# Transformer block, MLP stage: row moves on the sync queue in written order, later stores, and first inner sums made one stage earlier

## The chip, the cores and the metric

The kernel runs on one core of one Trainium2 chip. A core has TensorE (PE in the profile; its weight loads are PEld), VectorE (DVE), ScalarE (ACT), GpSimd (POOL) and SyncE (SP), and 16 DMA engines that they share. Each engine runs its own list of instructions in order and waits on semaphores for the others. DMAs are started by an instruction of SP, POOL or ACT; those of SP go into one hardware queue (q1 in the profile), those of POOL into a software queue (q0). The metric is the device time in microseconds of one execution; three runs of the kernel before gave 3164.5 to 3169.8 us, median 3166.41 us.

## The reference, cut to what matters

```python
mod = silu(c) @ w_ada + b_ada                         # six vectors of 576 per batch
x   = x + g_msa * (attention(ln(x) * (1 + sc_msa) + sh_msa) @ w_proj + b_proj)
xn2 = ln(x) * (1 + sc_mlp) + sh_mlp                   # x: 2 x 2048 rows of 576, float32
h   = gelu(xn2 @ w1 + b1)                             # w1: 576 x 2304
out = x + g_mlp * (h @ w2 + b2)                       # w2: 2304 x 576
```

Everything is float32. The change lies in the last three lines, the MLP; what is ahead of it (norms, attention with 16 heads of 36, projection) is the same in both kernels.

## The kernel before, in words

**First MLP half (`xn2`, `h`).** The 4096 rows are cut into 8 blocks `n` of 512 rows (`NB`), the 2304 hidden features into 2 times 9 chunks `f` of 128 (`HF` = 9). A job is one pair (n, f): it makes the chunk `f` of both feature halves for 512 rows, by Strassen's scheme in Winograd's form: seven products instead of eight for a 2 by 2 blocked product. There are 72 jobs, run two to a turn of the loop. Of a job, `whole_part` and `last_part` are TensorE's part (L1982, L1996); seven sums go to one PSUM side of three banks (`m0` or `m1`, jobs alternate) and a bank `one` that both sides share. `gelu_stored` (L2004 to L2026) then works on one of three SBUF tiles `cs0` to `cs2`, number job mod 3: ScalarE copies product 1 out of PSUM (L2008), VectorE adds up the rest (L2009 to L2016), ScalarE applies GELU to two halves (L2020), GpSimd makes the four sums of the hidden block that the second half needs (L2022 to L2025), and SP stores all seven 128x256 pieces, 896 KB, to `operands[n]` in DRAM (L2026). So PSUM of job j is wanted again by job j+2, and `cs` of job j by the ScalarE copy of job j+3.

**Rows for the next block.** While block m is worked on, the four 128-row tiles of block m+1 are made ready, by `ahead(job)`: *load* the rows from DRAM (L1026), *turn* them (layer norm by statistics on VectorE, a square root on ScalarE with its table load (L281), a scaling and a 32x32 transpose on VectorE (L1042), then four DMAs that write the squares to DRAM (L1047)), *read* the turned rows back (L1055, L1057: one DMA of 256 KB, two of 32 KB), and *modulate* them on ScalarE (L1064, L393, L394; six instructions). For tile i of block m+1 these stand at job 9m+2i plus an offset: load -5, turn -2, read 0, modulate 1. All its DMAs are GpSimd's. At a block's end `token_sums` (L1952 to L1955) makes the block's sums on VectorE.

**Weights for the second half.** `weights_made` cuts w2 into seven combinations with VectorE and keeps them in DRAM (`w_kept`): two of its 63 steps follow each two jobs. Each of four rounds of 13 steps has one step of four loads, one of three and one of four stores of 504 KB (L2073), all on SP, and eight of VectorE sums; a last, shorter round and the loading of the products 1, 2 and 6 into `w_first` follow.

**Second MLP half (`out`).** 56 products (n, m): for each block the seven outer Strassen products, each of which is again done by seven inner ones (`multiplied`, L2201 and L2210). The operand of a product, 1152 KB, is loaded from `operands` into one of three places in turn (L2125); its four inner sums (`sums_made`, L2183 to L2186) are made one product ahead, by GpSimd for even products and VectorE for odd ones. `combined_blocks`, `finished` and the branches between them add results up on VectorE and send four quadrants per block to `out` (L2247, on GpSimd).

**What sets the order.** Inside this part TensorE and VectorE follow the order of the code. The order on ScalarE, GpSimd and SP is chosen by the framework's scheduler, which places an instruction by what it estimates. Tiles are reused by address: `hs`, the pool of the second half, lies where the row blocks, the last rows of w1 and the `cs` tiles of the first half were, and a first write there waits for the last use.

## Time and profile before

The profiled execution took 3162.72 us, of which the span from its first to its last instruction is 3160.9 us. The table is of that execution. A job's or product's time is TensorE's, from its first matmul to that of the next.

| what | from | us |
|---|---|---|
| first MLP half, 72 jobs | 2122.86 to 2701.64 | 578.78 |
| a job when nothing is waited for (2666.64 to 2673.64) | | 7.00 |
| waits of TensorE in the first half, sum | | 51.7 |
| product 0 of the second half | 2701.64 to 2721.04 | 19.40 |
| a product when nothing is waited for (2721.04 to 2728.88) | | 7.84 |
| from the last matmul's end to the end of the span | 3152.41 to 3160.90 | 8.49 |

How to read the rows that follow: a row of the timeline has start and duration in us, engine, line, operation, written tile <- read tiles, the count of merged instructions (the duration then spans them all), and in brackets how long the engine had been idle and who released it. A row of a table by stage has the busy time of each engine, the granted TensorE clock as a share of the full one, the share of time in which the DMA engines were busy, and GB/s.

### The profile page before, as it was taken

The page shows a single profiled execution, that of the slowest core. Times are in us where ns is not written, and L with a number is a line of the kernel's source. Part 1 is how long each engine was busy: PE and PEld are TensorE (multiplying, and loading weights), DVE is VectorE, ACT ScalarE, POOL GpSimd, SP SyncE. Part 2 cuts the span into 40 slices and gives each one's busy share as a digit, 9 for nine tenths or more (in the row PEclk, how much of TensorE's full clock was granted, in tenths as well). Part 3 has the DMA queues.
Part 4 walks back from the last instruction along what each step waited for, and adds up shares of the span by engine and source line. Part 5 has one row for each costly group of instructions (what it writes and reads, how often), then busy time and mean ns, then how long its engine had stood idle before and what let it go on. Part 6 is the DMA issues. An engine that isn't in the chain of part 4 may idle for free.

```text
span 3160.9 us, 51170 instructions
## 1 busy us (share of the span) xinstructions
PE 3075.0 (97%) x19079; PEld 1917.0 (61%) x19079; DVE 1677.7 (53%) x2521; ACT 1493.4 (47%) x2909; POOL 1081.0 (34%) x1407
## 2 busy tenths in 40 slices
PE   8999999999999999999999999999888999899998
PEld 6883333333334788433333333378777878899998
DVE  6773444444444566434444434365555654576766
ACT  2336666766666033566666666614444543000000
POOL 4550100123321454100001111026666664555554
PEclk9999999999999999999999999999999999999999
DMA  5873332233342744311122222166776678765554
GB/s 151 189 139 88 100 88 57 74 94 91 95 112 55 230 89 81 79 45 44 46 55 80 80 65 74 33 201 175 216 225 186 184 223 286 278 201 191 202 188 144
DMA packets 368585, 413.53 MB, mean 131 GB/s; under 512 B 169288, under 2 KB 297864, under 8 KB 360200
## 3 DMA queue, kind: packets, MB, share of 16 engines
q1 hardware_dynamic: 311776, 286.35, 30.6%
q0 software_dynamic: 47120, 118.51, 14.2%
q10 hardware_dynamic: 9432, 5.31, 0.7%
q8 instruction: 153, 2.51, 0.3%
q14 instruction: 104, 0.85, 0.1%
HBM read 244.81 MB, written 154.75 MB: 126 GB/s over the span
## 4 chain that ended last, share of the span: by engine, by line
PE 81%; DMA 6%; POOL 4%; issue 3%; DVE 3%; ACT 3%; SPq 0%; POOLq 0%; DVEq 0%; ACTq 0%
PE b L1549 29%; PE b L1536 20%; PE b L2201 12%; PE s L1143 6%; PE s L1229 5%; PE m L1982 3%; DMA xnt<-turned 2%; PE s L411 2%; PE b L2210 2%; DMA parts<-turned 1%; DMA turned<-squares 1%; PE s L1145 1%; ACT cs L2020 1%; PE s L1235 1%; POOL cs L2023 1%
## 5 line engine op out<-in xcount | busy, mean ns | idle before, releaser
L1540 ACT ACTIVATE pt<-b 128x512 f32<-128x512 f32 x2048 | 1057.3, 610 | 482.1 <-PE b L1549 267.6
L1549 PE MATMUL b<-pt,vt 128*64 128x512 f32 x4096 | 935.0, 598 | 1.8 <-ACT pt L1540 1.8
L1549 PEld LDWEIGHTS b<-pt,vt 128*64 128x64 f32 x4096 | 271.8, 136 | 583.9 <-issue 437.7
L1536 PE MATMUL b<-qm,km 32*128 32x512 f32 x4096 | 563.8, 613 | 0.0
L1601 DVE TENSOR_TENSOR ot<-b,ot 128x512 f32<-128x512 f32 x192 | 132.8, 691 | 586.7 <-PE b L1549 586.7
L1536 PE MATMUL b<-qe,ke 16*128 16x512 f32 x2048 | 420.1, 791 | 0.0
L1536 PEld LDWEIGHTS b<-qm,km 32*128 32x128 f32 x4096 | 190.6, 184 | 271.2 <-ACT pt L1540 211.3
L1982 PE MATMUL m<-xnt,wb 128*128 128x256 f32 x864 | 217.0, 388 | 22.1 <-DVE cs L2016 21.2
L1143 PE MATMUL s<-wq,xnt 128*128 128x288 f32 x864 | 226.7, 406 | 2.0 <-ACT xnt L400 2.0
L1568 DVE RECIPROCAL den<-den 128x512 f32<-128x512 f32 x64 | 213.5, 3336 | 10.4 <-DMA den<-den_dram 10.4
L2218 ACT COPY one<-b 128x144 f32<-128x144 f32 x56 | 15.6, 278 | 425.1 <-PE b L2201 409.9
L1064 ACT ACTIVATE xnt<-xnt,mod 128x128 f32<-128x128 f32 x244 | 101.0, 482 | 238.2 <-DMA xnt<-turned 146.0
L1982 PE MATMUL m<-s,wb 128*128 128x256 f32 x864 | 210.9, 380 | 0.0
L1982 PEld LDWEIGHTS m<-xnt,wb 128*128 128x128 f32 x864 | 161.7, 194 | 47.3 <-DVE cs L2016 26.1
L1599 DVE COPY ot<-b 128x512 f32<-128x512 f32 x64 | 44.3, 692 | 273.5 <-PE b L1549 273.5
L1143 PEld LDWEIGHTS s<-wq,xnt 128*128 128x128 f32 x864 | 158.0, 190 | 37.5 <-ACT xnt L400 2.7
L1982 PEld LDWEIGHTS m<-s,wb 128*128 128x128 f32 x864 | 165.0, 191 | 22.7
L1536 PEld LDWEIGHTS b<-qe,ke 16*128 16x128 f32 x2048 | 106.7, 184 | 114.0 <-issue 113.3
L1658 POOL DMA_DIRECT2D spare<-in_x_dram x32 | 17.7, 554 | 442.7 <-DVE met L796 442.7
L2020 ACT ACTIVATE cs<-cs,b_sb 128x512 f32<-128x512 f32 x144 | 99.4, 719 | 106.0 <-DVE cs L2015 105.7
L2009 DVE TENSOR_TENSOR cs<-m,cs 128x512 f32<-128x512 f32 x72 | 49.2, 683 | 185.9 <-ACT cs L2008 145.7
L817 POOL DMA_DIRECT2D km<-qk x56 | 28.1, 502 | 322.8 <-PE b L1536 321.3
(305 smaller groups left out, 4672.0 us busy)
## 6 DMA issues: line engine op xcount, KB each, us to landing
operands<-cs SPq DMA_DIRECT2D x72, 896.0 KB
operand<-operands SPq DMA_DIRECT2D x37, 1152.0 KB
wb<-operands SPq DMA_DIRECT2D x19, 1152.0 KB
spare<-in_x_dram POOLq DMA_DIRECT2D x64, 288.0 KB, 3.1
x_dram<-spare POOLq DMA_DIRECT2D x64, 288.0 KB, 2.5
qm<-qk SPq DMA_DIRECT2D x256, 64.0 KB
den<-den_dram SPq DMA_DIRECT2D x128, 128.0 KB
w_kept<-w_first SPq DMA_DIRECT2D x31, 504.0 KB
```

Of the source, the lines that this page charges most:

```text
L411: nc.tensor.matmul(outs[a], stationary(k, a), moving(k, a), start=(first and k == 0), stop=(not first and k == FULL - 1),)
L1064: nc.scalar.activation(part, part, AF.Identity, **affine(which, k, b))
L1143: nc.tensor.matmul(out_a, full[:, k, :], wq[:, k, f], start=k == 0, stop=False)
L1229: nc.tensor.matmul(out[m], x_[:, k, :], w_(k), start=k == 0, stop=k == 1 and m == 6)
L1536: nc.tensor.matmul(ps, k[r, keys], q[r, :], start=first, stop=not first)
L1540: nc.scalar.activation(pt[:, h, :], banks[2 * c + h], AF.Exp, scale=SCALE)
L1549: nc.tensor.matmul(acc[64 * h : 64 * h + 64, :], vt[:, v0 : v0 + 64], pt[:, h, :], start=pt is pts[0][0], stop=pt is pts[-1][0],)
L1568: nc.vector.reciprocal(den, den)
L1601: nc.vector.tensor_tensor(ot, acc, ot, ALU.add)
L1982: nc.tensor.matmul(out_m[m], wb[:, f, slot[m], k, :], moving[m](k), start=k == 0 and m in (1, 2, 5, 6), stop=k == 1 and m == 1,)
L2020: nc.scalar.activation(part, part, AF.Gelu, bias=b1_sb[:, g : g + 1])
L2201: nc.tensor.matmul(out_m[m], stationary[m][:, c, :], w[:, FULL * (m - 1) + c, :], start=a == 0 and c == 0, stop=ends and c == FULL - 1 and ...
```

## The change

Six things are altered, all in the MLP.

1. Load, turn and read of the rows ahead go through SP instead of GpSimd, and modulate stands one job later (offset 2).
2. `gelu_stored` is split: `hidden_made` computes, and `hidden_stored`, which stores job j, is written two jobs later, behind the row moves of that place.
3. The loop of the first half is put under a manual schedule for SP, GpSimd and ScalarE: they follow the written order. SP also does in the second half.
4. The first three inner sums of product 0 are made by GpSimd in the first half, at job 36, in a tile of their own (`first_sums`); the fourth comes at the start of the second half, on VectorE.
5. The operand of product 1 is loaded in the first half, at job 64, to the front of the used-up weights `wb`; the weights of products 5 and 7 follow it there two jobs later than before (jobs 66 and 68), those of product 4 come behind product 1 of the second half, those of product 3 behind product 2.
6. The very last product has its own end, `last_finished`: its inner products 4 and 3 get a PSUM bank each, everything that doesn't need them is added first, and the two halves of the result leave separately through SP.

```diff
@@ rows ahead
-            for what, todo in at(turn=-2, read=0, modulate=1, load=-5):
+            for what, todo in at(turn=-2, read=0, modulate=2, load=-5):
-                    rows_ahead[todo] = mlp_loaded(*todo, nc.gpsimd)
+                    rows_ahead[todo] = mlp_loaded(*todo, nc.sync)
-                    rows_ahead[todo] = tile_turned(rows_ahead[todo], nc.gpsimd)
+                    rows_ahead[todo] = tile_turned(rows_ahead[todo], nc.sync)
-                    turned_loaded(block, cols, rows_ahead.pop(todo), nc.gpsimd)
+                    turned_loaded(block, cols, rows_ahead.pop(todo), nc.sync)
@@ stores
-            nc.sync.dma_start(out=operands[n][:, :, f, :].rearrange("i p c -> p i c"), in_=cs)
+        def hidden_stored(job):
+            if job >= 0:
+                n, f = divmod(job, HF)
+                nc.sync.dma_start(out=operands[n][:, :, f, :].rearrange("i p c -> p i c"), in_=css[job % 3])
@@ the loop (new text)
+        with tc.manual_schedule(
+            engines={mybir.EngineType.SP, mybir.EngineType.Pool, mybir.EngineType.Activation}
+        ):
+            for job in range(0, NB * HF, 2):
+                (n0, f0), (n1, f1) = divmod(job, HF), divmod(job + 1, HF)
+                ahead(job)
+                hidden_stored(job - 2)
+                whole_part(n0, f0, 0)
+                if f1 == 0:
+                    token_sums(n1)
+                last_part(n0, f0, 0)
+                ahead(job + 1)
+                hidden_stored(job - 1)
+                hidden_made(n0, f0, 0)
+                whole_part(n1, f1, 1)
+                last_part(n1, f1, 1)
+                if f1 == HF - 1 and n1 + 1 < NB:
+                    token_sums(n1 + 1)
+                hidden_made(n1, f1, 1)
+                for _ in range(2):
+                    if job >= 2 and making_weights:
+                        making_weights.pop(0)()
+                if job == 2 * HF:
+                    operand_loaded(0)
+                if job == 4 * HF:
+                    sums_made(0, slice(0, 3))
+                at_job = job + 1 - (NB - 1) * HF
+                if at_job == 2:
+                    operand_loaded(1)
+                for i, m in enumerate((5, 7)):
+                    if at_job == (4, 6)[i]:
+                        weights_loaded(m, weight_spots[m])
+        for job in (NB * HF - 2, NB * HF - 1):
+            hidden_stored(job)
@@ start of the second half
-        for i in (1, 2):
-            operand_loaded(i)
-        w_last = hs.tile([P, WSIZE], F32, name="w_last")
-        weights_loaded(3, w_last)
+        operand.append(hs.tile([P, HF, PAIR], F32, name="operand2"))
+        operand_loaded(2)
+        weight_spots[3] = hs.tile([P, WSIZE], F32, name="w_last")
+        sums[0].append(hs.tile([P, FULL, P], F32, name="fourth"))
+        sums_made(0, slice(3, 4))
@@ loop of the second half
+            quadrant = {2: (0, 0), 7: (1, 1), 4: (1, 0), 3: (0, 1)}.get(m)
+            xr = residual_rows(n, *quadrant, gate_bias) if quadrant else None
+            out_m, outs = multiplied(i)
+            operand_loaded(i + 3)
+            if i in (1, 2):
+                weights_loaded((4, 3)[i - 1], weight_spots[(4, 3)[i - 1]])
+            if i + 1 == len(products):
+                last_finished(z12, out_m, outs, n, *quadrant, xr, gate)
+                break
@@ end of the last product
+            tt(z, z, r, ALU.add)
+            tt(z, z, part, ALU.mult)
+            tt(z, z, xr, ALU.add)
+            for i, m, cols, op in ((1, 4, slice(0, QUARTER), ALU.subtract), (0, 3, slice(QUARTER, HALF), ALU.add)):
+                tt(r[:, i, cols], out_m[m], part[:, i, cols], ALU.mult)
+                tt(z[:, i, cols], z[:, i, cols], r[:, i, cols], op)
+                nc.sync.dma_start(out=rows_of(n, t, a, out)[:, i], in_=z[:, i])
```

What the built programs have at three places follows; tiles keep their numbers.

SP around job 18, block 2 (L2026 stores hidden blocks before, L2031 in the change). Before, SP carries stores and weights alone:

```order
L2026 DMA operands1_17603<-cs2_17979 128x7x256
L2026 DMA operands1_17603<-cs0_17977 128x7x256
L2026 DMA operands1_17603<-cs1_17978 128x7x256
L2026 DMA operands1_17603<-cs2_17979 128x7x256
L2026 DMA operands2_17604<-cs0_17977 128x7x256
```

In the change, the same stretch, from the read of one tile (`turned42`) at job 18 on:

```order
L1055 DMA xnt1_17620<-turned42_18768 128x4x128
L1057 DMA parts1_17621<-turned42_18768 64x128 x2
L1047 DMA turned43_18869<-squares_18867 32x18x32 x4
L2031 DMA operands1_17603<-cs1_17979 128x7x256
L1026 DMA xt1_17971<-x1_dram_190 128x576
L2031 DMA operands1_17603<-cs2_17980 128x7x256
L2152 DMA operand0_17965<-operands0_17602 128x2304
L1055 DMA xnt1_17620<-turned43_18869 128x4x128
L1057 DMA parts1_17621<-turned43_18869 64x128 x2
L1047 DMA turned44_18968<-squares_18966 32x18x32 x4
L2031 DMA operands2_17604<-cs0_17978 128x7x256
```

The store of job 16 (`cs1`) now stands behind the four writes of a turn; that of job 17 (`cs2`) has only a load ahead of it. In blocks of even number a turn stands in the first half of a loop turn, ahead of both stores; in blocks of odd number it stands between the two.

ScalarE early in block 0 (jobs 4 and 5, `cs1` and `cs2`). Before:

```order
L281 ACT_TABLE_LOAD
L281 ACTIVATE std_18189<-mv_18187,eps6_65 128x1
L1064 ACTIVATE xnt1_17620<-xnt1_17620,mod_91 128x128 x4
L393 ACTIVATE parts1_17621<-parts1_17621,mod_91 128x128
L394 ACTIVATE tail1_17622<-parts1_17621,mod_91 128x128
L2008 COPY cs1_17978<-one_17985 128x256
L2020 ACT_TABLE_LOAD
```

In the change:

```order
L1064 ACTIVATE xnt1_17620<-xnt1_17620,mod_91 128x128 x4
L393 ACTIVATE parts1_17621<-parts1_17621,mod_91 128x128
L394 ACTIVATE tail1_17622<-parts1_17621,mod_91 128x128
L281 ACT_TABLE_LOAD
L281 ACTIVATE std_18190<-mv_18188,eps6_65 128x1
L2009 COPY cs1_17979<-one_17986 128x256
L2021 ACT_TABLE_LOAD
```

Before, the tile that is modulated here was read back by a DMA of the preceding job; in the change its read belongs to job 2, two jobs earlier, and the modulation stands ahead of the root of the next turn.

GpSimd at the handover to the second half (operand0 is product 0's operand, operand2 product 2's; `cs2` holds job 71). Before:

```order
L2025 TENSOR_TENSOR cs2_17979<-cs2_17979 128x256
L2183 TENSOR_TENSOR sums_21336<-operand0_17965 128x512
L2185 TENSOR_TENSOR sums_21336<-operand0_17965 128x512
L2184 TENSOR_TENSOR sums_21336<-sums_21336,operand0_17965 128x512
L2186 TENSOR_TENSOR sums_21336<-operand0_17965,sums_21336 128x512
L2183 TENSOR_TENSOR sums_21395<-operand2_21331 128x512
```

In the change:

```order
L2026 TENSOR_TENSOR cs2_17980<-cs2_17980 128x256
L2146 TENSOR_TENSOR first_sums_17966<-operand2_21340 128x512 x2
L2146 TENSOR_TENSOR first_sums_17966<-first_sums_17966,operand2_21340 128x512
L2146 TENSOR_TENSOR fourth_21343<-operand2_21340,first_sums_17966 128x512
```

Product 0's sums are gone from this place; the next thing GpSimd does is product 2's.

More of the change, by code (lines that the diff above doesn't have):

```diff
@@ L1938, in block_of_small @@
         operand = [m2.tile([P, HF, PAIR], F32, name="operand0")]
+        first_sums = m2.tile([P, 3, FULL, P], F32, name="first_sums")
         close_xs = token_tiles(3)
@@ L2119, in block_of_small, with operand_parts, sums_made @@
         spots = wb.rearrange("p f m k c -> p (f m k c)")
+        operand.append(spots[:, 0 : HF * PAIR].rearrange("p (f c) -> p f c", f=HF))
+        weight_spots = {
+            m: spots[:, HF * PAIR + i * WSIZE : HF * PAIR + (i + 1) * WSIZE] for i, m in enumerate((5, 7, 4))
+        }
+        sums = {0: [first_sums[:, j] for j in range(3)]}
+        def operand_parts(i):
+            x_ = operand[i % 3]
+            return (x_[:, FULL * k : FULL * (k + 1), t * P : (t + 1) * P] for t in range(2) for k in range(2))
+        def sums_made(i, which):
+            a11, a12, a21, a22 = operand_parts(i)
+            of = sums[i % 2]
+            engine = nc.vector if i % 2 or which.start == 3 == which.stop - 1 else nc.gpsimd
+            for op in (
+                (of[0], a21, a22, ALU.add),
+                (of[1], of[0], a11, ALU.subtract),
+                (of[2], a11, a21, ALU.subtract),
+                (of[3], a12, of[1], ALU.subtract) if len(of) > 3 else None,
+            )[which]:
+                engine.tensor_tensor(*op)
         products = [(n, m) for n in range(NB) for m in (1, 2, 6, 5, 7, 4, 3)]
@@ L2193, in multiplied @@
             out_m, outs = {}, {}
-            for group in ((1,), (2, 6), (5, 7), (4, 3)):
+            last = ((4, 3),) if i + 1 < len(products) else ((4,), (3,))
+            for group in ((1,), (2, 6), (5, 7), *last):
                 ps = bank()[:, 0 : 2 * QUARTER].rearrange("p (a f) -> p a f", a=2)
```

76 lines of the change are left out of this document (27 added, 49 removed).

## The prediction

> **What bounds the kernel now.** The time by stage comes first, since the change touches only the MLP. The rows are the first half up to its last wait, its end, product 0 of the second half, products 1 to 55, and the tail.
>
> ```profile
> 2122.86:2637.38 514.52, 462.79 (x2259) 402.86 (x2260) 298.06 (x480) 246.33 (x429) 331.56 (x490) 0.97 0.69 200
> 2637.38:2701.64 64.26, 64.26 (x335) 57.65 (x334) 25.72 (x40) 16.18 (x28) 28.32 (x39) 1.00 0.94 345
> 2701.64:2721.04 19.40, 10.97 (x66) 10.76 (x65) 8.16 (x10) 1.55 (x3) 8.53 (x9) 0.74 1.00 387
> 2721.04:3152.41 431.37, 431.37 (x3522) 431.15 (x3520) 302.49 (x500) 15.33 (x55) 228.54 (x171) 1.00 0.57 192
> 3152.41:3160.90 8.49, 0.00 (x0) 0.00 (x0) 3.10 (x6) 0.00 (x0) 0.72 (x1) 0.67 0.12 41
> ```
>
> TensorE bounds nearly everything: 55 of the 56 products run without a gap, so all that this change can win lies in the first, third and last of these stages. In the second of them a job takes 7.00 us, so 72 jobs would take 504.0; they take 514.52 + 64.26 = 578.8. Lost: 74.8 us, of which 514.52 - 462.79 = 51.7 idle, the other 23.1 in slower matmuls. Who holds TensorE up, first by the table of waits, then by that of the tile `xnt`:
>
> ```profile
> PE one L1982 <- ACT cs L2008: 30.5, 18, 4.2
> PE m L1982 <- DVE cs L2016: 21.2, 23, 4.5
> PE b L2201 <- POOL sums L2184: 8.4, 1, 8.4
> ...
>   DMA xnt<-turned: 117.7, 27
> DMA to landing us min/median/max: 3.3/5.7/8.0
> ```
>
> TensorE waits for evictions, but these aren't too much work (ScalarE is busy 246 of 515 us). ScalarE sat idle 117.7 us, 27 times, 4.36 us on average, for rows that were still being read back. The timeline shows one such case, then the longest wait:
>
> ```profile
> 2162.90 1.65 ACT L1064 ACTIVATE xnt<-xnt,mod 128x128 f32<-128x128 f32 x4 [3.99 <-DMA xnt<-turned]
> 2164.45 0.48 ACT L393 ACTIVATE parts<-parts,mod 128x128 fp32r<-128x128 f32 x1
> 2165.22 0.35 ACT L2008 COPY cs<-one 128x256 f32<-128x256 f32 x1
> 2165.62 2.07 PE L1982 MATMUL one<-xnt,wb 128*128 128x256 f32 x4 [2.35 <-ACT cs L2008]
> 2167.63 0.69 DVE L2016 TENSOR_TENSOR cs<-cs,m 128x512 f32<-128x512 f32 x1
> 2337.38 3.78 PE L1982 MATMUL m<-xnt,wb 128*128 128x256 f32 x8 [4.51 <-DVE cs L2016]
> ```
>
> The copy at 2165.22 could not pass the modulation ahead of it in ScalarE's list, and TensorE waited for the copy. Eight matmuls after the 4.51 us wait took 3.78 us where eight take 1.89 in the steady stretch below: a long wait costs a slow stretch behind it. Over the half, 23.1 / 51.7 = 0.45 us of slowness goes with each idle us. The Trainium skill ("TensorE: Matmul & The Clock Gate", Part 1: The HAM clock gate) puts half rate behind an idle window of about 3.4 us. This trace shows the like after 2.35 us already (2.07 us for four matmuls, half of 3.78 for eight); by that page waits under 3.4 us would cost no more than themselves, and the remainder forecast below some 3 us less.
>
> **Row moves and the later modulation.** With offset 2, ScalarE comes to a tile 7.00 us later than now, against a mean wait of 4.36. The read's issue must then not slip by more than 2.6 us on average, and SP's list is fuller. The steady rhythm first, job start T = 2666.64:
>
> ```profile
> 2666.64 1.89 PE L1982 MATMUL m<-xnt,wb 128*128 128x256 f32 x8
> 2668.88 0.69 DVE L2016 TENSOR_TENSOR cs<-cs,m 128x512 f32<-128x512 f32 x1
> 2668.93 1.39 ACT L2020 ACTIVATE cs<-cs,b_sb 128x512 f32<-128x512 f32 x2 [2.63 <-DVE cs L2015]
> 2672.93 0.37 ACT L2008 COPY cs<-one 128x256 f32<-128x256 f32 x1 [2.61 <-PE one L1982]
> 2673.32 7.36 SPq L2026 DMA_DIRECT2D operands<-cs  x2
> ```
>
> The previous job is evicted by T+2.93 and through GELU by T+3.68; this job's copy starts at T+6.29. After an eviction's end two weight sums of about 1.3 us (a row below) stand on VectorE, so SP, in order behind the weights' stores, reaches a read at about T+6, and ScalarE the tile at T+14+3.7. That leaves 11.7 us for a landing of at most 8.0. The 30.5 and 21.2 us should go where this alone caused them.
>
> **Stores behind turns: the new wait.** Now the store of the previous job is issued at T+6.7, and its buffer wanted 13 us later. In the change the store of job k-2 follows the turn of loop turn k in blocks of even number; copy k+1, which writes the same buffer, is due at T+13.3. The turn's links:
>
> ```profile
> 2173.07 1.28 DVE L2083 TENSOR_TENSOR w_first<-w_first 128x576 f32<-128x576 f32 x1
> 2157.31 1.28 ACT L281 ACT_TABLE_LOAD   x1
> 2213.21 0.29 ACT L281 ACTIVATE std<-mv,eps 128x1 f32<-128x1 f32 x1 [1.75 <-DVE mv L279]
> 2214.51 0.78 DVE L1042 STREAM_TRANSPOSE squares<-x_first 128x576 f32<-128x576 f32 x1
> L1312 SPq DMA_DIRECT2D qk<-turned_qk x112: 303/517/1532, 1110.7 to 1288.8; - x112
> 2311.18 6.53 SPq L2073 DMA_DIRECT2D w_kept<-w_first  x4
> ```
>
> From GELU's end: modulation 1.65 + 0.48 + 0.48 = 2.61, table 1.28, root 0.29, then 1.79 to the transposes' end (2213.50 to 2215.29), so T+9.65. Four writes on SP are not in this trace for these tiles; the nearest rows, 72 KB each on SP from an earlier stage, give 0.517 each (0.303 to 1.532), 2.07, so the store goes at T+11.7. Its landing has no row. Below it is 896 KB at the 345 GB/s of the second stage, 2.66, plus an issue of about 0.36; above, the longest landing of rows, 8.0. I take 3.5, near the lower end, since the rows' writes are small; where three or four weight stores run ahead (6.53 us for SP to issue four) 7.5. Copy and eviction then take 3.10 (2165.22 to 2168.32), to T+18.3 where T+16.93 is due: late by 1.4 us, of 4.07 that PSUM's two sides allow (eviction is needed at T+21). But the lateness is carried to the next loop turn. Without a modulation table and root could come 2.6 us earlier; VectorE's weight sums and statistics hold them back, and I take 1.2 earlier, so that a plain landing adds 0.2 and is neglected.
>
> Even blocks have turns at 4 loop turns each (3 in block 0), 15 in all; modulations meet 7, weight stores precede those at jobs 22, 36, 38 and 52. Lateness by these prices: block 2: 0, 0, 1.4, then 1.4 + 5.4 = 6.8, a stall of 2.7. Block 4: 0, 4.1, 9.5, a stall of 5.4, then 1.4 more. Block 6: 4.1, 4.1, then two stalls of 1.4. Sum 12.3 us idle, with 0.45 of slowness 18. Add 4 for starts and block ends, whose waits (part of the 21.2) the change doesn't touch: 22 of the 74.8 stay, **52.8 gained**; between 5 (no chain) and 45 (landings near 8.0 everywhere) staying. The Trainium skill ("DMA: Bandwidth & Descriptors", Queues, rings and completion order) speaks against this change: an engine consumes one ring in order, and takes turns between queues. By it a store, so far beside the rows, must run wholly behind them.
>
> GpSimd loses 27 loads, turns and reads, which win time only for its own sums, off the path; the three sums at job 36, about 4 us, lie in its spare time (331.56 of 514.52 busy). Without that cover they would delay one store by 4 us, once.
>
> **The handover.**
>
> ```profile
> 2702.14 0.51 SPq L2125 DMA_DIRECT2D wb<-operands  x1
> 2708.24 1.26 POOL L2183 TENSOR_TENSOR sums<-operand 128x512 f32<-128x512 f32 x1
> 2708.83 0.44 SPq L2125 DMA_DIRECT2D operand<-operands  x1
> 2710.33 0.93 DVE L2183 TENSOR_TENSOR sums<-wb 128x512 f32<-128x512 f32 x1 [5.77 <-DMA wb<-operands]
> 2710.68 1.71 POOL L2184 TENSOR_TENSOR sums<-sums,operand 128x512 f32<-128x512 f32 x1
> 2712.44 6.07 PE L2201 MATMUL b<-w_first,sums 128*128 128x144 f32 x24 [8.43 <-POOL sums L2184]
> 2723.25 3.10 PE L2201 MATMUL b<-w_first,sums 128*128 128x144 f32 x24
> 2728.88 2.12 PE L2201 MATMUL b<-w_first,operand 128*128 128x144 f32 x16
> ```
>
> Product 0 takes 19.40 us, a later one 7.84 (2721.04 to 2728.88): 11.56 lost, 8.43 of it waiting for sums that GpSimd could begin only behind job 71's, and most of the rest slow matmuls (6.07 against 3.10). With three sums ready this goes. Late next is product 2: its operand still follows job 71's store on SP, issued at about 2708.8. The operand issued at 2702.14, also behind a store, had landed 8.2 us later. Three GpSimd sums (1.26 + 1.26 + 1.71) bring the needed one to 2721.2 at worst; product 2 starts at 2701.64 + 15.68 and wants it 2.4 us on, at 2719.7. So 0 to 1.5 stays: **10.5 gained**. Product 1's sums on VectorE (about 3 us from 2705) end before 2709.5. The weights of products 4 and 3 now start 16 and 24 us into the half, wanted 39 and 47 us in; at 192 GB/s, 2232 KB take 11.9, covered.
>
> **The tail.**
>
> ```profile
> 3149.99 0.46 DVE L2224 TENSOR_TENSOR r<-b,r 128x288 f32<-128x288 f32 x1 [1.68 <-PE b L2210]
> 3152.00 0.41 PE L2210 MATMUL b<-w_last,wb 128*128 128x144 f32 x2
> 3152.44 0.30 DVE L2225 TENSOR_TENSOR r<-r,b 128x144 f32<-128x144 f32 x1 [1.99 <-PE b L2210]
> 3154.99 0.76 DVE L2246 TENSOR_TENSOR r<-r,xr 128x576 f32<-128x576 f32 x1
> 3156.05 0.72 POOL L2247 DMA_DIRECT2D out_dram<-r  x1 [7.12 <-DVE r L2246]
> ```
>
> VectorE's new list from 3150.45: two of 0.30, three of 0.76, four of 0.30 and about 0.08 between them, done at 3155.2 instead of 3155.75. The last store then leaves by SP: 3160.90 - 3156.05 = 4.85 as now at most, 2.7 (SP's issue 0.36 plus 2.3) if SP lands faster. Gain 0.5 to 3; I take **2**.
>
> Sum: 52.8 + 10.5 + 2 = 65.3. The profiled execution took 3162.7; 3097.4. The median of the runs is 3.7 above it: **3101 us**.
>
> **The rivals.** *No chain*: landings of 3 us or less and shared overlap leave no stall. For it: DMAs are busy only 0.69 of the first stage. Against: weights' stores bunch. Then 74.8 + 11.5 + 3 go: 3077. *The reads stay late*: SP, held by turns and weight stores, issues reads more than 2.6 us later, so ScalarE waits as now; the half stays at 578.8 and 12.5 are gained: 3154. For it: SP's turn writes wait for VectorE; against: the 11.7 us computed. *One queue sets the pace* (slower): each of the 15 store-after-turn places adds its landing to the loop. It outweighs the 12.5 + 74.8 when each costs 5.8 us, that is from a landing of about 8 us on; at 11 us, 15 times about 8 us with slow matmuls is 174, less 87: about 3253. For it: at 7.00 us a job the first stage's 62.8 jobs take 440 us, in which its transfers, busy 0.69 x 515 us now, need 0.81 of the DMA time. Against: 8.0 is the longest landing seen, and weight stores precede only four places.
>
> **How the numbers follow.** Forecast 0.57, no chain 0.22, late reads 0.14, slower 0.07. The forecast's own range, 5 to 45 staying, is 3083 to 3125; with no chain below and some of the late reads above, 8 times in 10 lie in 3077 to 3135. A measurement here tells 0.2% (6.3 us) from no change: faster 0.90, within 0.04, slower 0.06.
>
> **What would show it.** Waits of ScalarE for `xnt` from 117.7 to under 20 us; jobs of 7.0 us in odd blocks; TensorE's remaining idle time in even blocks, where ScalarE's copy waits for a store; granted clock near 1.00. Product 0 near 7.9 us, the tail near 6.5. I am wrong if waits are spread evenly over blocks, if `xnt` still heads ScalarE's waits, or if products 1 to 55 grow beyond 431.4.

## The result, and the profile after

The changed kernel takes 3114.09 us (median of 4 runs, 3113.41 to 3120.5), the kernel before on the same chip 3165.45 us (3162.74 to 3169.8). The ratio is 0.9841, with a 95% interval of 0.9824 to 0.9858: faster by 1.6%. Forecast were 3101 us in a range of 3077 to 3135.

The stages first, from the table by stage of the changed kernel: first half, product 0, products 1 to 55, tail. Columns as in the table of before.

```profile
2122.76:2660.83 538.07, 513.42 (x2593) 454.66 (x2593) 307.45 (x519) 260.68 (x457) 238.87 (x318) 0.99 0.77 233
2660.83:2668.66 7.83, 7.83 (x66) 7.83 (x65) 7.37 (x10) 1.55 (x3) 4.00 (x4) 1.00 0.35 120
2668.66:3104.34 435.68, 432.14 (x3522) 431.31 (x3520) 304.72 (x506) 15.37 (x55) 228.31 (x172) 1.00 0.57 205
3104.34:3111.40 7.06, 0.00 (x1) 0.00 (x0) 2.05 (x6) 0.00 (x0) 0.00 (x0) 0.71 0.16 49
```

The first half fell from 578.78 to 538.07 us, a gain of 40.7; the second from 450.77 (19.40 + 431.37) to 443.51 (7.83 + 435.68), 7.3; the tail from 8.49 to 7.06, 1.4. The sum, 49.4, is the difference of the spans (3160.9 and 3111.4). Of the 74.8 us that the first half had lost against 72 jobs of 7.00 us, 34.1 are left, 24.7 of them idle. The table of waits says who holds TensorE up now:

```profile
ACT cs L2009 <- DMA operands<-cs: 70.3, 17, 11.0
PE m L1983 <- DVE cs L2017: 17.0, 18, 1.6
PE one L1983 <- ACT cs L2009: 7.7, 5, 2.8
PE b L2232 <- POOL first_sums L2146: 2.4, 1, 2.4
```

ScalarE's wait for rows, 117.7 us before, is gone from the table. In its place stands a wait that before did not have: 70.3 us in which ScalarE's copy could not write `cs` because an older store still read it. One case of it in block 2, from the timeline:

```profile
2286.73 2.16 SPq L2078 DMA_DIRECT2D w_kept<-w_first  x3
2293.00 2.51 SPq L1047 DMA_DIRECT2D turned<-squares  x4
2295.61 1.23 SPq L2031 DMA_DIRECT2D operands<-cs  x2
2301.23 0.37 ACT L2009 COPY cs<-one 128x256 f32<-128x256 f32 x1 [5.59 <-DMA operands<-cs]
2301.65 1.13 PE L1983 MATMUL one<-xnt,wb 128*128 128x256 f32 x4 [1.27 <-ACT cs L2009]
```

SP issues three stores of weights, then (behind moves of rows that are left out here) the four writes of a turn, and only then two stores of hidden blocks; the copy comes 5.6 us after the first of these, which it waits for, and TensorE after the copy. This is the chain that the prediction called "stores behind turns". Most of it lies where it was forecast. The waits of TensorE in the stretches of blocks 2, 4 and 6 (2252 to 2320, 2387 to 2457, 2522 to 2589), two rows each:

```profile
PE m L1983 <- DVE cs L2017: 3.2, 3, 1.6
PE one L1983 <- ACT cs L2009: 1.3, 1, 1.3
PE m L1983 <- DVE cs L2017: 4.2, 5, 1.6
PE one L1983 <- ACT cs L2009: 3.4, 2, 2.7
PE m L1983 <- DVE cs L2017: 4.5, 5, 1.6
PE one L1983 <- ACT cs L2009: 0.2, 1, 0.2
```

That is 4.5, 7.6 and 4.7, together 16.8 of the 24.7. The rest is 5.1 in blocks 1, 3 and 5, of which 3.7 stand behind their first jobs, and, in block 7, one wait that nobody had forecast:

```profile
2607.44 2.51 SPq L2118 DMA_DIRECT2D w_first<-w_kept  x3
2609.99 0.68 SPq L2152 DMA_DIRECT2D wb<-operands  x1
2613.90 10.87 SPq L2031 DMA_DIRECT2D operands<-cs  x2
2624.86 7.35 SPq L2118 DMA_DIRECT2D wb<-w_kept  x1
2635.92 0.37 ACT L2009 COPY cs<-one 128x256 f32<-128x256 f32 x1 [11.03 <-DMA operands<-cs]
2636.35 2.07 PE L1983 MATMUL one<-xnt,wb 128*128 128x256 f32 x4 [2.78 <-ACT cs L2009]
```

The copy is job 67's and waits for the store of job 64, the first of the two at 2613.90, which lands 22.0 us later. Two things could hold it: the load of product 5's weights, which is issued 11 us behind it but shares the DMA engines and keeps SP for 7.35 us, or the three loads for `w_first` and product 1's operand ahead of it, 3 x 2232 + 1152 = 7848 KB issued in 3.2 us. The experiments and their traces decide.

At the handover product 0 no longer waits; products 2 and 3 do, and 3.5 us are lost there (2.42 and 0.94 in waits for sums, 0.18 for none that the profile shows):

```profile
2669.38 0.55 SPq L2152 DMA_DIRECT2D operand<-operands  x1
2676.89 3.03 POOL L2146 TENSOR_TENSOR first_sums<-operand 128x512 f32<-128x512 f32 x2 [7.95 <-DMA operand<-operands]
2681.71 3.21 PE L2232 MATMUL b<-w_first,first_sums 128*128 128x144 f32 x24 [2.42 <-POOL first_sums L2146]
```

### The profile page after: what moved, and what is told of

Same layout as the page of the kernel before. It is cut to its first block, busy times and chain, and to the rows that moved or that the text cites. A ratio compares the mean times of both kernels' runs of the same rounds, so it can differ in the third digit from the quotient of the medians.

```text
span 3111.4 us, 51193 instructions
## 1 busy us (share of the span) xinstructions
PE 3059.0 (98%) x19079; PEld 1909.4 (61%) x19079; DVE 1661.6 (53%) x2525; ACT 1491.8 (48%) x2909; POOL 954.1 (31%) x1191
## 3 DMA queue, kind: packets, MB, share of 16 engines
q0 software_dynamic: 35968, 94.02, 11.2%
## 4 chain that ended last, share of the span: by engine, by line
PE 85%; DMA 4%; DVE 4%; ACT 3%; SPq 2%; issue 1%; POOL 1%; DVEq 0%; ACTq 0%; POOLq 0%
PE b L1549 29%; PE b L1536 20%; PE b L2232 12%; PE s L1143 6%; PE s L1229 5%; PE m L1983 4%; PE s L411 4%; DMA operands<-cs 3%; PE b L2241 2%; SPq L1047 1%; PE s L1145 1%; PE m L1997 1%; PE s L1235 1%; PE one L1983 1%; ACT xnt L1064 1%
## 5 line engine op out<-in xcount | busy, mean ns | idle before, releaser
L1064 ACT ACTIVATE xnt<-xnt,mod 128x128 f32<-128x128 f32 x244 | 99.9, 481 | 116.7 <-DMA weight_sums<-sums_kept 50.8
L2023 POOL TENSOR_TENSOR cs<-cs 128x256 f32<-128x256 f32 x72 | 59.5, 826 | 294.1 <-ACT cs L2021 294.1
```

The source lines that it names most:

```text
L1064: nc.scalar.activation(part, part, AF.Identity, **affine(which, k, b))
```

## The experiments

The first half is told from TensorE's first matmul of it to the first of product 0, the second from there to its last matmul's end. In the diffs, minus and plus stand against the kernel named ahead.

The waits for rows are those for `xnt`. "Read to modulation" is the time from the issue of a tile's read (L1055) to the start of its modulation (L1064), the median of the 27 tiles.

| kernel | first half | second half | read to modulation | ScalarE waits for rows | for stores | time (median) |
|---|---|---|---|---|---|---|
| before | 578.8 | 450.8 | 5.7 | 117.7 | 0 | 3165.5 |
| changed | 538.1 | 443.5 | 15.0 | 0 | 70.3 | 3114.1 |
| stores first | 514.2 | 443.5 | 11.6 | 2.6 | 25.9 | 3092.6 |
| before, offset 2 only | 574.2 | 450.6 | 5.7 | 118.2 | 0 | 3160.0 |
| changed, rows on GpSimd | 524.2 | 443.2 | 10.0 | 0 | 40.7 | 3101.3 |
| changed, offset 1 | 534.4 | 443.3 | 8.3 | 28.1 | 37.9 | 3113.5 |
| before, order only | 615.8 | 465.3 | 7.9 | 126.1 | 20.1 | 3217.0 |
| before, order and offset 2 | 517.2 | 465.1 | 10.0 | 1.3 | 25.1 | 3118.0 |
| stores first, offset 1 | 553.4 | 443.3 | 6.5 | 70.7 | 22.0 | 3130.3 |

The traces enter the first half between 2122.7 and 2125.8 us, though nothing ahead of it differs. Times of two kernels less than 3 us apart therefore say little, and the two halves say more.

### Stores ahead of the row moves

Against the changed kernel:

```diff
-                ahead(job)
                 hidden_stored(job - 2)
+                ahead(job)
...
-                ahead(job + 1)
                 hidden_stored(job - 1)
+                ahead(job + 1)
```

> The changed kernel with one thing turned round: in each loop turn the store of an older job stands ahead of the row moves of that place, not behind them. Theory (a store that stands behind a turn reaches its buffer too late for the next ScalarE copy): ScalarE's waits for operands<-cs fall from 70.3 us to under 15, TensorE's idle time in the first half from 24.7 to about 10, and the time from 3114 to about 3095 (3088 to 3102). Rival (rows and stores share one queue, wherever each stands in the list, so the transfers hold each other up in any order): the waits stay above 50 us and the time within 5 us of 3114.

Measured 3092.56 us (3091.98 to 3093.51), ratio 0.9773 (0.9757 to 0.979). Its waits:

```profile
ACT cs L2009 <- DMA operands<-cs: 25.9, 6, 10.8
PE m L1983 <- DVE cs L2017: 5.3, 7, 1.5
PE one L1983 <- ACT cs L2009: 2.6, 1, 2.6
```

TensorE's idle time in the first half falls from 24.7 to 7.9 us, the half from 538.1 to 514.2. So the order of store and turn on SP cost the change 21.5 us, and the chain is shown. ScalarE's waits for stores fell less than expected, to 25.9 us and not under 15; the longest of them, 10.8, is the one in block 7, which stays.

### The later modulation alone

Against the kernel before: `modulate=1` becomes `modulate=2`.

> The kernel before with modulate at offset 2 in place of 1 and nothing else: rows still move on GpSimd, the scheduler still orders ScalarE, GpSimd and SP. If the later modulation alone brings the first half's gain (40.7 us), about 3125 (3117 to 3135), with ScalarE's waits for xnt falling from 117.7 us to under 20. If the written order or the sync queue brings a good part of it, 3140 or more.

Measured 3160.03 us (3158.0 to 3163.18), ratio 0.9986 (0.9977 to 0.9996), and ScalarE waits as long as ever:

```profile
ACT xnt L1064 <- DMA xnt<-turned: 118.2, 27, 6.6
```

The traces show why: under the scheduler the edit did not move the modulation. It starts 9.9 us (median) behind the start of the job that its read is written for, where the kernel before has 9.3 and the kernels with the written order and offset 2 have 17.6 to 18.3; the first three tiles are modulated in jobs 3, 5 and 7, as before, and not in 4, 6 and 8. In this run a read issued at 2231.16 is modulated at 2237.62; in the kernel before one issued at 2229.08 is modulated at 2236.18. So the run doesn't test a later modulation. It shows that the offset does nothing as long as the scheduler orders ScalarE, which the prediction had not said.

### Rows back on GpSimd

Against the changed kernel: `nc.sync` becomes `nc.gpsimd` in the load, the turn and the read of `ahead`.

> The changed kernel with load, turn and read of the rows put back on GpSimd, in written order; stores stay late and modulate stays at 2. Theory: no store waits behind a turn on SP any more, so the copies' waits for stores fall under 15 us and the time to about 3097 (3090 to 3105); GpSimd's own sums wait for the turns' transposes, off the path. Rival (transfers hold each other up): two queues take turns, the total of the transfers is the same, within 5 us of 3114.

Measured 3101.26 us (3100.35 to 3102.87), ratio 0.9802 (0.9785 to 0.9818); ScalarE's waits for stores fall from 70.3 to 40.7 us. The time is in the range expected, the waits are not under the 15 us expected. So SP's queue isn't needed for the gain; it costs 13 us as long as stores follow the turns in it.

### Offset 1 in the changed kernel

Against the changed kernel: `modulate=2` becomes `modulate=1`.

> The changed kernel with modulate back at offset 1. Theory (the later modulation is what takes ScalarE's wait for reads away): ScalarE waits for xnt again, 27 times some 3 to 5 us (80 to 130 us), TensorE's idle time in the first half is back at 45 to 60 us, 3140 (3128 to 3155). Rival (order and queue had made the reads earlier, the offset is not needed): within 6 us of 3114.

Measured 3113.49 us (3111.56 to 3117.32), ratio 0.9844 (0.9828 to 0.986): no difference from the changed kernel, as the rival had it and not the theory. 28.1 us of waits for rows come back, but waits for stores fall from 70.3 to 37.9 us; TensorE idles 21.3 us instead of 24.7. With the chain in the way, the offset seems only to decide which of two waits ends last; the run with offset 1 and the stores first, below, fits this.

### The order alone, and the order with offset 2

Against the kernel before:

```diff
+        with tc.manual_schedule(engines={mybir.EngineType.SP, mybir.EngineType.Pool, mybir.EngineType.Activation}):
-        for job in range(0, NB * HF, 2):
+            for job in range(0, NB * HF, 2):
...
```

> The kernel before with one thing of the change: SP, GpSimd and ScalarE follow the written order in the first half. Rows still move on GpSimd, modulation stands one job behind the read, a store stands right behind its GELU; second half and tail as before. Theory, formed after the later modulation alone left ScalarE 118.2 us waiting for rows: it is the order of the lists that decides, since the scheduler had put the reads of rows behind GpSimd's own sums, right ahead of the modulation that wants them. Then ScalarE's waits for rows fall below 30 us, the first half from 578.8 to 520 to 540 us, and with handover and tail as before (19.4 and 8.5 us) the time is 3107 to 3125 us. Rival: it is the move from GpSimd's queue to SP's that brings the rows in time; then the waits stay above 80 us and the time lies within 3150 to 3168 us.

Measured 3216.96 us (3215.84 to 3219.28), ratio 1.0171 (1.0155 to 1.0186): slower than before. Neither expectation had that. Waits, and one case from the timeline:

```profile
ACT xnt L1064 <- DMA xnt<-turned: 126.1, 16, 10.2
PE one L1982 <- ACT cs L2008: 75.5, 16, 6.6
```

```profile
2186.58 0.75 POOL L1055 DMA_DIRECT2D xnt<-turned  x1
2193.16 1.65 ACT L1064 ACTIVATE xnt<-xnt,mod 128x128 f32<-128x128 f32 x4 [8.79 <-DMA xnt<-turned]
2195.88 2.08 PE L1982 MATMUL one<-xnt,wb 128*128 128x256 f32 x4 [4.74 <-ACT cs L2008]
```

In written order the read stands behind the sums of the job ahead on GpSimd, and the modulation one job on, ahead of the copy that TensorE needs: there are fewer waits than before (16, not 27) but of 7.9 us each instead of 4.4. The next run adds offset 2 to this, and nothing else.

> The kernel before with two things of the change and nothing else: the written order on SP, GpSimd and ScalarE in the first half, and modulation two jobs behind the read. Rows stay on GpSimd, stores right behind their GELU. Alone, the order made it slower (3217 us, ScalarE waiting 126 us for rows), and offset 2 did nothing (3160 us, 118 us). Theory: the two only work together. In written order a read stands behind the sums of the job ahead on GpSimd, some 7 us into its job, so one job is too short for it and two are enough. ScalarE's waits for rows fall below 15 us, the first half takes 515 to 535 us instead of 578.8, handover and tail stay: 3103 to 3122 us. Rival: the later stores and SP's queue are needed too, since on GpSimd the writes of a turn hold up the sums that a store needs; then TensorE still waits for ScalarE's copies and the time is above 3135 us.

Measured 3118.01 us (3115.83 to 3119.55), ratio 0.9852 (0.9837 to 0.9867). The waits for rows:

```profile
ACT xnt L1064 <- DMA xnt<-turned: 1.3, 1, 1.3
```

A read at 2235.24 is now modulated at 2248.12, 12.9 us later (median of all tiles 10.0), and the half takes 517.2 us: these two edits, of which alone one wins 0.1% and the other loses 1.7%, win 61.6 of the 74.8 us, without SP and without later stores. With the rest of the change (rows on SP, stores two jobs later and behind turns, loads and sums moved into the half) it is 538.1. The time is no better than 3118 us because the handover is the old one, and lost more in product 3 (below).

### Offset 1 with the stores first

Against the changed kernel: both edits, stores first and `modulate=1`.

> The changed kernel with the stores ahead of the row moves on SP, and with modulation one job behind the read as before the change. Theory: with stores out of the way offset 2 takes the last waits for rows away, so offset 1 brings some back: ScalarE waits 20 to 35 us for rows (28.1 with stores behind the turns, 2.6 with stores first and offset 2), and some of it reaches TensorE: 3095 to 3102 us against 3092.6. Rival: the offset does nothing for the time once the stores go first: 3091 to 3094.5 us, with any waits for rows covered.

Measured 3130.33 us (3129.3 to 3131.72), ratio 0.9896 (0.9881 to 0.9911):

```profile
ACT xnt L1064 <- DMA xnt<-turned: 70.7, 18, 11.5
PE one L1983 <- ACT cs L2009: 26.9, 13, 10.7
```

The offset is worth 38 us here, more than the 2 to 9 expected, and nothing with the stores behind the turns. The traces agree with a reason that is plain from the lists: a store on SP waits for GpSimd's sums, so a read behind it goes out later, 4.3 us (median) into the job that it is written for, against 0.1 with offset 1 and the stores behind the turns. That leaves 6.5 us to the modulation instead of 8.3. Where a read stands in the list decides how late the modulation must be.

### The sums of product 0 at the handover

Against the version with stores first:

```diff
-                if job == 4 * HF:
-                    sums_made(0, slice(0, 3))
...
-        sums_made(0, slice(3, 4))
+        sums_made(0, slice(0, 4))
```

> The changed kernel with the stores first, but product 0's inner sums are made at the start of the second half, on GpSimd, as before the change. Theory of the prediction: GpSimd is busy with job 71's sums until some 8 us after product 0's start, three more sums follow, and product 0 wants its first sum 2.4 us in: it takes 18 to 20 us instead of 7.8, and with the 3.4 us that products 2 and 3 now wait partly hidden behind that, the time is 3100 to 3104 us. Rival: the wait only moves, because product 2's operand is late in either case: less than 5 us more, 3092.6 to 3097 us.

Measured 3094.92 us (3091.61 to 3095.84), ratio 0.9779 (0.9764 to 0.9794). This run does not test what it was meant to: behind the ordered loop the scheduler chooses again, and it put the first three sums back to 2272.9 us, right behind the operand's load; only the fourth stood at the handover, for a wait of 2.28 us. It shows that a tile of its own was enough for the first three sums to be made early. The repeat puts the sums where the old ones were, in the pool `hs`, whose space is free only behind job 71:

```diff
-        first_sums = m2.tile([P, 3, FULL, P], F32, name="first_sums")
...
+        sums_even = hs.tile([P, 4, FULL, P], F32, name="sums_even")
+        sums[0] = [sums_even[:, j] for j in range(4)]
+        sums_made(0, slice(0, 4))
```

> The changed kernel with the stores first, but product 0's four sums go to a tile of the pool hs, as before the change, so that GpSimd can make them only behind job 71's sums. (The earlier run of this kind had kept their own tile, and the scheduler had put three of them back at job 20.) Theory of the prediction: product 0 wants its first sum 2.4 us in and gets it some 10 us in; it takes 18 to 20 us instead of 7.8; less the 3.4 us of products 2 and 3, which are covered meanwhile, 7 to 9 us more: 3099 to 3102 us. Rival: the wait only moves, because product 2's operand is late in either case: less than 5 us more, 3092 to 3097 us.

Measured 3103.72 us (3099.92 to 3106.34), ratio 0.9812 (0.9797 to 0.9827). Product 0 waits again, and products 2 and 3 no longer do:

```profile
2651.54 5.23 PE L2230 MATMUL b<-w_first,sums_even 128*128 128x144 f32 x24 [9.12 <-POOL sums_even L2145]
2659.30 2.12 PE L2230 MATMUL b<-w_first,wb 128*128 128x144 f32 x16
```

Product 0 takes 19.24 us (2640.06 to 2659.30), the second half 450.6 instead of 443.5: 7.1 us by the traces, as expected, 11.2 by the medians, above the 7 to 9 expected, with runs that scatter over 6 us here. The rival falls. The early sums are worth 7 to 11 us, and the prediction had 10.5 for the whole handover.

### What is left: two edits, then the loads spread, then in thirds

Against the version with stores first: product 5's and 7's weights are loaded by GpSimd, and product 2's operand goes to a free place of `wb`, ahead of the last store; product 4's and 3's weights follow one product later.

> The changed kernel with the stores first, and two more edits for the waits that are left there: the weights of products 5 and 7 are loaded by GpSimd instead of SP, where the first of them held a store 7.1 us (ScalarE waited 10.85 us for it, TensorE 2.6 and 0.6), and product 2's operand goes ahead of job 71's store, to a place in the used-up weights wb that is free after job 70 (products 2 and 3 waited 2.4 and 0.9 us; the weights of product 4, which had that place, come one product later, those of 3 too). Theory: both waits go, with their slow matmuls 4 + 3.4 us: 3085 us (3083 to 3088). Rival: loads of 2232 KB share the DMA engines with the store from whichever queue they come, so the store is late all the same and only the handover is won: 3088 to 3090.5 us.

Measured 3091.98 us (3090.59 to 3092.6), ratio 0.9772 (0.9759 to 0.9786): nothing won, which neither expectation had. The copy in block 7 still waits 10.4 us for its store, and the handover has a new wait (below). The next version keeps the place of product 2's operand, but takes product 7's weights out of the first half, loads product 5's at job 68 by SP, and fetches residual rows one product earlier (from its diff against the version with stores first):

```diff
-                for i, m in enumerate((5, 7)):
-                    if at_job == (4, 6)[i]:
-                        weights_loaded(m, weight_spots[m])
+                if at_job == 6:
+                    weights_loaded(5, weight_spots[5])
...
+            if i + 1 < len(products):
+                rows_loaded(i + 1)
             operand_loaded(i + 3)
-            if i in (1, 2):
-                weights_loaded((4, 3)[i - 1], weight_spots[(4, 3)[i - 1]])
+            if i in (0, 2, 3):
+                m_next = {0: 7, 2: 4, 3: 3}[i]
+                weights_loaded(m_next, weight_spots[m_next])
```

> The changed kernel with the stores first and the loads around the handover spread out: of the weights only those of product 5 are loaded in the first half (job 68), those of product 7 behind product 0, those of 4 and 3 behind products 2 and 3; product 2's operand goes between the stores of jobs 70 and 71, to a place in the used-up weights wb; and the residual rows of a product are fetched one product earlier, ahead of the next operand. Theory: what is left at the end of the first half is transfers of 2232 KB meeting stores, and what is left of the handover is product 2's operand behind job 71's store and VectorE waiting for residual rows; both go, about 4 and 3.4 us of the 3092.6: 3085 us (3083 to 3088). Rival: a load of 2232 KB ahead of any store makes that store late, and the loads moved behind the handover make new waits there: 3089 to 3094 us.

Measured 3086.36 us (3085.56 to 3092.08), ratio 0.976 (0.9747 to 0.9774): the fastest version. TensorE has no wait left in the second half (439.2 us; 56 products of 7.84 are 439.0):

```profile
2637.12:3076.40 439.28, 439.20 (x3586) 438.99 (x3584) 297.97 (x515) 16.86 (x58) 226.06 (x175) 1.00 0.59 211
```

The time lies in the range expected, but only half of the theory came: the second half won 4.3 us (443.5 to 439.2), the first 0.4 (514.2 to 513.8). The wait in block 7 stays: its copy waits 10.6 us, TensorE 2.35. The last version cuts product 5's weights in three loads of 744 KB, at jobs 66, 68 and 70.

> As the run with the loads spread out, but the weights of product 5 are loaded in three pieces of 744 KB, at jobs 66, 68 and 70, instead of one of 2232 KB at job 68. Theory: the last stall of the first half, 2.35 + 0.62 us after a copy that waited 10.6 us for a store, comes from the length of the load ahead of that store; a third of it delays a store by a third, which the three tiles cs and PSUM's two sides absorb. The stall and its slow matmuls go: 3082 to 3085 us against 3086.4, ScalarE's longest wait for a store below 7 us. Rival: any load ahead of a store costs it a landing of its own, whatever its size; three such loads then make three stalls, 3086 to 3092 us.

Measured 3087.52 us (3085.32 to 3089.68), ratio 0.9757 (0.9744 to 0.9771), the same as the one before. SP and the copy:

```profile
2586.67 2.52 SPq L2118 DMA_DIRECT2D w_first<-w_kept  x3
2593.14 10.93 SPq L2031 DMA_DIRECT2D operands<-cs  x2
2604.17 6.96 SPq L2192 DMA_DIRECT2D wb<-w_kept  x1
2614.55 0.37 ACT L2009 COPY cs<-one 128x256 f32<-128x256 f32 x1 [10.42 <-DMA operands<-cs]
2621.81 0.55 SPq L2192 DMA_DIRECT2D wb<-w_kept  x1
```

The theory falls, and so does the rival's reason, though the time lies in its range: there is one stall and not three. A third of the load holds SP as long as the whole did (6.96 us), the next third 0.55, so that length isn't the load's own. Nor does the load hold up the store. The copy, job 67's, writes the tile of job 64, whose store went out at 2593.14, ahead of the load, and landed 21 us later. In the version with the loads spread the same copy came at 2612.90, after 10.6 us of waiting, and product 5's weights only after it:

```profile
2620.19 0.51 SPq L2118 DMA_DIRECT2D wb<-w_kept  x1
```

So the weights of product 5, which the last three expectations blamed, are not the cause. What stands ahead of that store in all versions of the change are the 7848 KB for `w_first` and product 1's operand. The DMA records of the traces tell the transfers apart by the size of their packets, and on SP's queue these begin in the order of issue. In this run the 384 packets of 17856 bytes for `w_first` run from 2590.2 to 2607.8, the operand's 128 of 9216 bytes from 2606.3 to 2611.7, and the first of the store's 1024 bytes begins at 2609.7, 16.5 us after the store's issue; the first third of product 5's weights begins at 2614.4. In the changed kernel the same four begin at 2610.9, 2627.1, 2630.2 and 2635.0. So the store is late because it stands behind these loads on the queue: between 2590 and 2600 us the DMA engines move 433 GB/s, at which 7848 KB and the store alone take some 20 us. In the kernel before, the scheduler had put the loads for `w_first` between stores, at 2641, 2647 and 2659 us; in written order they follow each other. What spreading them would win was not run.

## Why the prediction was right, and where it wasn't

**The new wait** was forecast in its mechanism, its place and nearly its size: 12.3 us idle in blocks 2, 4 and 6 (2.7, 6.8 and 2.8), measured 16.8 (4.5, 7.6 and 4.7). The turn's writes took about what was put in (2.0 to 2.6 us at nearly all places of the even blocks, against 2.07). Two terms were off, in opposite directions, so that the sum came nearer than its parts. The plain landing was too small: 3.5 us taken, 4.3 to 4.9 measured, 6.0 and 6.2 at two places. So places that were neglected ("adds 0.2") added up. A plain one, in block 2:

```profile
2278.64 1.09 SPq L2031 DMA_DIRECT2D operands<-cs  x2
2282.97 0.37 ACT L2009 COPY cs<-one 128x256 f32<-128x256 f32 x1 [1.92 <-DMA operands<-cs]
```

The landing behind weight stores was too large: 7.5 us taken, 4.7 to 5.6 measured at the four places (5.6 is the case in block 2 above); what such stores cost more is the time that they hold the turn itself up, as at 2517.65, where its four writes took 5.07 us. What jobs lost beyond idle time is 9.4 of the 34.1 us, 0.38 for each idle us, where 0.45 was used; 4.1 of it fell on jobs 40, 41 and 68 with matmuls at about half speed, the rest is small losses at each wait. The sum that stays, 22 forecast, is 16.8 + 5.1 + 2.8 idle and these 9.4; the 4 put in for starts and block ends compare with the 5.1 of the odd blocks. By the rule of the Trainium skill that the prediction quoted ("DMA: Bandwidth & Descriptors", Queues, rings and completion order) an engine consumes one ring in order; the packets in block 7 agree. ("Wholly behind", in the prediction, is more than the page has, which leaves open that a later transfer finishes first.) That stores first win 21.5 us and rows in GpSimd's queue 12.8 fits, but doesn't tell the ring from SP's own list, which is in order too.

**The cause of the gain was told by half.** "With offset 2, ScalarE comes to a tile 7.00 us later" is true only where the lists follow the written order; the prediction doesn't name the manual schedule as a condition of it. Offset 2 alone gained 0.1%, since the scheduler left the modulation where it was; the order alone lost 1.7%, since the reads went out later (6.8 us into their job, median, against 3.6); both together won 61.6 us of the first half. The forecast 52.8 came out near 40.7 because it was made on the row of waits that had to vanish, and it did (117.7 to 0); that the change met the condition was luck, as far as the argument goes. What makes it work is the distance from read to modulation: 11.7 us were worked out against a longest landing of 8.0, and the medians are 15.0 in the changed kernel, 11.6 with the stores first and 10.0 with order and offset 2 alone, where little or no waiting is left, but 5.7 to 8.3 in the five kernels that wait.

**The late reads** (3154 us) and **no chain** (3077) didn't come; **one queue sets the pace** didn't either, since the landings behind turns (4.3 to 6.2 us) stayed under the 8 us from which it decides. The prediction missed that written order also bunches the weights: 2.8 us idle in block 7.

**The handover** was right for product 0 (7.83 us, "near 7.9") and late by the second step: of 10.5 us 7.3 came. Product 2's operand landed 7.5 us after its issue, where 8.2 was put in, but it was issued 8.6 us into the half and not 7.2, and GpSimd's three sums took 4.8 (2676.89 to 2681.71) where 1.26 + 1.26 + 1.71 was put in, so 0 to 1.5 us became 2.4. That product 3 would wait for VectorE, which stood behind residual rows that stood behind these sums and then took 4.71 us for one sum (below), was not seen. With this a sign came that the prediction had given for being wrong: products 1 to 55 grew from 431.37 to 435.68 us. The **tail** gained 1.4 of 2 (7.06 us where "near 6.5" was said), by the rows

```profile
3106.03 0.91 SPq L2299 DMA_DIRECT2D out_dram<-r  x2
3106.26 0.31 DVE L2298 TENSOR_TENSOR r<-r 128x144 f32<-128x144 f32 x1
```

VectorE ends at 3106.57, 2.2 us after the last matmul (2.8 forecast: 3155.2 against 3152.41). From there to the end it is 4.8 us, as from GpSimd before (4.85), so SP's store landed at the slow one of the two bounds.

## What to carry to other kernels

Where a hand-written order replaces a scheduler's, price the distance from each transfer's issue to its first use in the list as it will stand, for each engine: an offset that is too short in one order is enough in another, an edit of the text does nothing where a scheduler still chooses the place, and two edits that are useless or harmful alone can be most of the gain together. Measure that distance in the trace before a run without gain is taken to refute the idea. On a queue that carries both what somebody soon waits to overwrite and what is needed much later, put the first ahead; that swap of two lines was worth 21.5 of the 73 us that the stores-first version wins. And look at what the new order bunches, not only at what it moves.

## What the runs showed of the hardware

VectorE's sum of two SBUF tiles, 0.69 us by itself, took 4.7, 7.3 and 10.1 us where GpSimd began a run of instructions just behind it. The longest, from the run with order and offset 2:

```profile
2680.97 0.68 DVE L2184 TENSOR_TENSOR sums<-operand 128x512 f32<-128x512 f32 x1
2681.68 10.09 DVE L2185 TENSOR_TENSOR sums<-sums,operand 128x512 f32<-128x512 f32 x1
2682.12 1.27 POOL L2185 TENSOR_TENSOR sums<-sums,wb 128x512 f32<-128x512 f32 x1
2685.77 5.45 POOL L2239 TENSOR_TENSOR xr<-xr,gate 128x576 f32<-128x576 f32 x4
2691.83 5.79 PE L2202 MATMUL b<-wb,sums 128*128 128x144 f32 x24 [11.21 <-DVE sums L2185]
```

VectorE, which had started 0.44 us ahead of GpSimd's first, ended its sum at 2691.77, after GpSimd's whole run (2691.22), and TensorE waited 11.2 us for it, in product 3. The Trainium skill ("SBUF — State Buffer", Who interferes with whom) has the rule that such a sum contends with a GpSimd instruction that reads SBUF, and that the loser blocks for the whole instruction. The traces agree that it blocks, and show more: it blocked through several GpSimd instructions on end. The sum of 4.7 us stands in the changed kernel and with the stores first too, where product 3 waited 0.94 us for it. In the version with GpSimd's weight loads, product 2 no longer waited, product 3 came earlier to the same late sum and waited 2.98 us, and 23 matmuls behind that took 5.89 us, where 24 take 3.21 in the changed kernel: that is where most of this version's gain went (446.4 us in the second half against 443.5).

Nor does the length of a wait alone decide whether slow matmuls follow. Four matmuls took 2.07 us after 2.35 us idle in the kernel before and after 2.78 in the changed one, but the normal 1.13 after 2.88 with rows on GpSimd, after 2.35 with the loads spread, and after 2.60 with the stores first:

```profile
2616.17 1.13 PE L1983 MATMUL one<-xnt,wb 128*128 128x256 f32 x4 [2.60 <-ACT cs L2009]
```
